# A PSUM pool for the scores, and the q and k projections in the common ring: an attention kernel on one core

## The chip, the core and the metric

The kernel runs on one core of one Trainium2 chip. The metric is the device time of one execution in microseconds (us). Times come from several executions of the compiled program; the profile comes from one further execution, taken by the hardware profiler. The engines are called PE (matmul), PEld (PE's weight loads), DVE, ACT, POOL and SP (which issues DMAs).

## What is computed

For x of 8 batches x 512 tokens x 128 channels in f32, the output is x plus two functions of xn, the layer norm of x:

```
x + rel_attention(xn) + local_transformer(xn)

rel_attention: 16 heads of 8 dims, causal, with a table of relative
               positions for keys and one for values
local_transformer, 6 times:
    y = shift_tokens(x)                 # half of the channels one token back
    q, k, v = split(y @ Wqkv)           # 16 heads of 64 dims
    q, k = l2norm(q) * qs, l2norm(k) * ks, then rotary with scales
    sim = 8 * q k^T in windows of 32: each looks at itself and the one before
    x = x + softmax(sim) v @ Wo
    z = layernorm(shift_tokens(x)) @ W1 ; a, gate = split(z)      # 341 wide each
    x = x + (a * gelu(gate)) @ W2
```

## The kernel before, in words

`rel_attention` does the first part, up to about 560 us of the span. Everything after it, and a beginning that runs beside the end of it, is `steps_of_layers`: 6 layers x 8 batches x 4 tiles of 128 tokens, one tile after another. The state `xt` stays in SBUF, transposed (channels on the partitions). A **batch** here is four tiles and one feed-forward.

A tile passes through these steps. The letters are those of the written order further down.

- `p0` to `p3`, `project` (from L739): half of q, of q, of k, of k. Three matmuls into one bank, `qk_ps` (L637 to L639: the operands are split in a high and a low part, and `product` adds three of the four products). DVE reads the bank twice (`q` L762, `rot` L763), ACT once (`sq`, L764). After the second half, POOL adds `q` and `rot` (L767) and sums of squares are made: for q by POOL L769 and DVE L770, for k by DVE L772, both into `ss`.
- `r`, `normalise` (L777): DVE makes the reciprocal root of `ss` (L782, then L70 to L81; an intermediate, `root_ps`, lies in PSUM too), and POOL multiplies q and k by it (L786).
- `q0 q1 k0 k1`, `turn` (L800): four transposes on PE into one bank, `qkT_ps` (L805), and a copy by ACT into `qT` or `kT` (L808).
- `s0 s1`, `scores` (L810): a matmul that writes the mask into one bank, `sc_ps` (L824), and 32 pairs of small matmuls on top (L836). DVE takes the maximum (L844) and ACT eight exponentials out of the bank, each with its sum (L857). After `s1` DVE inverts the sums (L873), POOL multiplies (L874) and DVE transposes (`pT`, L876).
- `v0` to `v3`, `values` (L881): `product` with Wv and Wo joined, into `v_ps`; a copy by ACT (L890), and four DMAs from SP (L892) that put it in rows of windows, `vw`.
- `a0 a1`, `attend` (L897): matmuls of `vw` and `pT` into `y_ps` (L910), which is held from `a0` to `a1`; a copy by ACT, `ys` (L921).
- `+`, `add` (L924): a transpose into `yT_ps` (L928), added to `xt` by DVE in two parts (L931).
- `f`, `feed_forward` (from L933), once a batch, in stages: the mean over channels by two matmuls with ones (`mean_ps`, L945 and L946; L945 therefore starts once a batch), DVE L947, the square by ACT L949, `var_ps` L953, the reciprocal root by DVE on 4 columns (L76 to L81, then `rstd_hi` L965 and `rstd_lo` L966), `dg` by POOL (L971, twice), `rstd_ps` L978, DVE L986 and L990, ACT L989; then `gate_ps` and `val_ps` (three of each, by `product`), ACT's gelu `h` (L1001), DVE L1011, the split of `h` (ACT L625, POOL L626), `f_ps` by nine matmuls (L1026), and DVE's add to `xt` (L1035, twice). In the last layer `fin_ps` (L1045) follows.

At a layer's end the next layer's weights come by DMA and are split into high and low parts: ACT makes the high parts (L625), DVE most of the low ones (L626, among them `wqk_lo`).

**Orders.** PE's order is written by hand. It is the table ORDERS (L48 to L53), one row for each tile of a batch, run under `tc.manual_schedule`. The first and third rows read

```
"p0 p1 v0 f s0 w2 + p2 f p3 q0 f f q1 s1 w2 k0 v1 w1 a0 r a1 w1 k1 v2 v3"
"p0 p1 s0 w2 v0 v1 f p2 q0 q1 p3 s1 w2 k0 w1 + a0 r a1 w1 k1 v2 v3"
```

In step n of the loop, `p` and `r` belong to tile n + 2, `q` and `k` to tile n + 1, `s` and `v` to tile n, `a` to tile n - 1 and `+` to tile n - 2; `w` loads or splits weights. The orders of DVE, ACT and POOL are not written: the builder's planner chooses them as it builds, from its own model of the timeline, and it also chooses which buffer of a pool a tile takes.

**Banks.** PSUM has eight banks here, and each tile named `..._ps` takes one. `PSB = (2, 6)`. Two banks are the pool `b_qk` (L596), for `qk_ps` alone. Six are the pool `b_x` (L1085), a ring under the one tag `x`, for everything else: `sc_ps`, `qkT_ps`, `v_ps`, `y_ps`, `yT_ps`, the feed-forward's tiles and the roots'. The first instruction that writes a tile waits for the last one that reads the tile which had the bank before (`reuse_waits="tile"`). `rel_attention` has banks of its own while it runs; `b_x` is opened when these are free. Until then `steps_of_layers` has `b_qk` and, through the dictionary `spare`, a pool of `rel_attention` for roots. It projects the first two tiles in that time.

Of the kernel before, what the change touches and what calls it, by code (L numbers as in the profile page):

```python
# [11 lines left out]
F32 = mybir.dt.float32  # L12
# [6 lines left out]
PSUM = bass.MemoryType.PSUM  # L19

P = 128
# [20 lines left out]
H, D = 16, 64  # L42
INNER = H * D
W = 32
# [9 lines left out]
PSB = (2, 6)  # L54
VAR = {'Z': '', 'N': '', 'C': '0', 'D': 1, 'hl': 'P', 'xl': 'P', 'fl': 'P', 'v': 'AAAA', 'q': 'AA', 'k': 'AA', 'pr': 'P', 'R5': 0, 'lo2': 'V'}
NW = P // W
# [526 lines left out]
def local_layers(tc, i, ident, ident_b, xt, out, spare):  # L583


    with ExitStack() as ctx:
        yield from steps_of_layers(ctx, tc, i, ident, ident_b, xt, out, spare)


def steps_of_layers(ctx, tc, i, ident, ident_b, xt, out, spare):  # L590
    nc = tc.nc

    def pool(name, bufs, **kw):
        return ctx.enter_context(tc.tile_pool(name=name, bufs=bufs, reuse_waits="tile", **kw))

    ps_qk = pool("b_qk", PSB[0], space=PSUM, side="right")  # L596
    wp = pool("b_w", 2, side="right")
    w1p = pool("b_w1", 1, side="right")
    w3p = pool("b_w3", 3, side="right")
# [4 lines left out]
    def eng(c):  # L604
        return nc.gpsimd if c == "P" else nc.vector
# [4 lines left out]
    def in_turn(step):  # L610


        ins = step.ins
        if "any" in last:
            tc.add_manual_dep(
                ins,
                last["any"].name,
                mybir.DependencyInfo(mybir.DependencyClass.NoSync, mybir.DependencyReason.DATA),
                reason="one table at a time",
            )  # L620
        last["any"] = ins
# [11 lines left out]
    def product(ps, lhs, rhs):  # L633


        (ah, al), (bh, bl) = lhs, rhs
        nc.tensor.matmul(ps, lhsT=ah, rhs=bh, start=True, stop=False)  # L637
        nc.tensor.matmul(ps, lhsT=ah, rhs=bl, start=False, stop=False)  # L638
        nc.tensor.matmul(ps, lhsT=al, rhs=bh, start=False, stop=True)  # L639
# [96 lines left out]
    def halves(xs, t):  # L736
        return [x[:, t * P : (t + 1) * P] for x in xs]

    def project(n, c):  # L739

        part, a = divmod(c, 2)
        l, b, t = tiles[n]
        if c == 0:
            ready[n] = {"ss": pq.tile([P, 2, H], F32, name="ss")}
        if a == 0:
            ready[n][part] = [
                pq.tile([P, H, 2, D // 2], F32, name="q", bufs=4),
                pq.tile([P, H, 2, D // 2], F32, name="rot", bufs=3),
                pq.tile([P, 2, H, D // 2], F32, name="sq"),
            ]  # L750
        q, v, sq = ready[n][part]
        xs, w, ss = streams[l, b], projections[l, part], ready[n]["ss"]
        cos, sin = (
            tables[l, t][:, 2 * part + m, :].rearrange("p (a d) -> p a d", a=2) for m in range(2)
        )

        def wide(x):
            return x.unsqueeze(1).to_broadcast([P, H, D // 2])

        ps = ps_qk.tile([P, H, D // 2], F32, name="qk_ps")  # L760
        product(ps.rearrange("p h d -> p (h d)"), halves(xs, t), w[a])
        nc.vector.tensor_mul(q[:, :, a], ps, wide(cos[:, a, :]))  # L762
        nc.vector.tensor_mul(v[:, :, 1 - a], ps, wide(sin[:, 1 - a, :]))  # L763
        nc.scalar.activation(sq[:, a], ps, AF.Square)  # L764
        if a == 0:
            return
        nc.gpsimd.tensor_add(q, q, v)  # L767
        if str(part) in VAR["C"]:
            nc.gpsimd.tensor_add(sq[:, 0], sq[:, 0], sq[:, 1])  # L769
            nc.vector.tensor_reduce(ss[:, part, :], sq[:, 0], AX.X, ALU.add)  # L770
        else:
            nc.vector.tensor_reduce(  # L772
                ss[:, part, :], sq.rearrange("p a h d -> p h a d"), AX.XY, ALU.add
            )
        ready[n][part] = q.rearrange("p h a d -> p h (a d)")
# [34 lines left out]
    def scores(n, p):  # L810


        t = tiles[n][2]
        if p == 0:
            probs[n] = {
                "pr": p2.tile([P, 2, 2, NW, 2 * W], F32, name="pr"),
                "mx": p2.tile([P, 2, 2, NW], F32, name="mx"),
                "sm": p2.tile([P, 2 * 2 * NW], F32, name="sm"),
            }
        pr, mx, sm = (probs[n][k] for k in ("pr", "mx", "sm"))  # L820
        qT, kT = turned[n]["q"], turned[n]["k"]
        mask = masks[:, 0 if t == 0 else 1].rearrange("p w k -> p (w k)")
        ps = ps_x.tile([P, 2, NW, 2 * W], F32, name="sc_ps", tag="x")
        nc.tensor.matmul(  # L824
            ps.rearrange("p g w k -> p g (w k)"),
            lhsT=ident_b,
            rhs=mask.unsqueeze(1).to_broadcast([P, 2, NW * 2 * W]),
            start=True,
            stop=False,
            skip_group_check=True,  # L830
        )
        r = slice(D * p, D * p + D)
        for g in range(2):
            for w in range(NW):
                for j in range(4):
                    nc.tensor.matmul(  # L836
                        ps[32 * j : 32 * j + 32, g, w, :],
                        lhsT=qT[r, 4 * g + j, W * w : W * w + W],
                        rhs=kT[r, 4 * g + j, W * w : W * w + 2 * W],
                        start=False,  # L840
                        stop=(g, w) == (1, NW - 1),
                        skip_group_check=True,
                    )
        nc.vector.tensor_reduce(mx[:, p], ps, AX.X, ALU.max, negate=True)  # L844
        if str(p) in VAR["Z"]:
            nc.vector.tensor_add(
                pr[:, p], ps, mx[:, p].unsqueeze(3).to_broadcast([P, 2, NW, 2 * W])
            )
            in_turn(nc.scalar.activation(pr[:, p], pr[:, p], AF.Exp))
        for g in range(2):  # L850
            for w in range(NW):
                if str(p) in VAR["Z"]:
                    continue
                m = (2 * p + g) * NW + w
                kw = {} if str(p) in VAR["N"] else dict(accum_out=sm[:, m : m + 1])
                in_turn(
                    nc.scalar.activation(  # L857
                        pr[:, p, g, w, :],
                        ps[:, g, w, :],
                        AF.Exp,  # L860
                        bias=mx[:, p, g, w : w + 1],
                        **kw,
                    ),
                )
        if str(p) in VAR["Z"] + VAR["N"]:
            nc.vector.tensor_reduce(
                sm[:, 8 * p : 8 * p + 8], pr[:, p].rearrange("p g w k -> p (g w) k"), AX.X, ALU.add
            )
        if p == 0:
            return  # L870
        del turned[n]
        flat = pr.rearrange("p a g w k -> p (a g w) k")
        nc.vector.reciprocal(sm, sm)  # L873
        eng(VAR["pr"]).tensor_mul(flat, flat, sm.unsqueeze(2).to_broadcast([P, 16, 2 * W]))  # L874
        pT = p2.tile([P, 2, 2, NW, 2, W], F32, name="pT")
        nc.vector.transpose(  # L876
            pT.rearrange("p a g w b q -> p (a g w b q)"), pr.rearrange("p a g w k -> p (a g w k)")
        )
        probs[n] = pT
# [193 lines left out]
    for n in range(2):  # L1073
        for c in range(4):
            project(n, c)
            if c == 3:
                normalise(n)
            yield
# [3 lines left out]
    p2 = pool("b_p2", 2)  # L1082
    p3 = pool("b_p3", 3)
    vp = pool("b_vw", 9)
    ps_x = pool("b_x", PSB[1], space=PSUM)  # L1085
    spare.update(pool=ps_x, tag="x")


    mask_f = p1.tile([P, 2, NW, 2 * W], F32, name="mask_f", tag="fsq")
# [11 lines left out]
    with tc.manual_schedule(engines={nc.tensor.engine}):  # L1101
        for n in range(-1, len(tiles) + 2):
# [10 lines left out]
            for step in ORDERS[n % NT].split():  # L1113
# [8 lines left out]
                elif kind == "r" and more:  # L1122
                    normalise(n + 2)
                elif kind == "q" and have(n + 1):
                    turn_q(n + 1, k)
                elif kind == "k" and have(n + 1):
                    turn_k(n + 1, k)
                elif kind == "s" and have(n):
                    scores(n, k)
                elif kind == "v" and have(n):  # L1130
                    values(n, k)
                elif kind == "a" and have(n - 1):
                    attend(n - 1, k)
                elif kind == "+" and have(n - 2):
                    add(n - 2)
                    l, b, t = tiles[n - 2]
                    if t == NT - 1:
                        if l not in weights:
                            weights[l] = load(l)
                        feeding = feed_forward(l, b, weights[l])  # L1140
                elif kind == "f":
                    next(feeding, None)
                elif kind == "w":

                    if have(n + k) and tiles[n + k][1:] == (0, 0):
                        next(making, None)
# [95 lines left out]
```

## Time and profile before

| | us |
|---|---|
| six runs | 3543.26 to 3552.78 |
| median of them | 3549.32 |
| the profiled execution | 3547.9 |
| its span, from the first to the last instruction | 3546.2 |

All shares are of the span. PE is busy for 94% of it, PEld for 71%, DVE for 86%, ACT for 81% and POOL for 83%; TensorE's granted clock is 0.98 in the mean. In an ordinary stretch of 60 us in the layers (2221 to 2281 us) PE is busy 58.80 us, PEld 45.78, DVE 53.72, ACT 52.37 and POOL 54.89, at a granted clock of 1.00.

Rows of the waits view read "engine, line <- releaser: us in all, times, longest": the engine stood still ahead of that line's instruction, and the releaser's end let it go. Rows of the timeline read "start, length, engine, line, operation, output <- inputs, shapes", with the idle time ahead of it and its releaser in brackets. The chain is followed back from the last instruction, at each step to what released it; its shares say on which engine the time of that one path lies.

### The profile page before, as it was taken

To read this page: it belongs to the slowest core of one execution; us is meant where nothing else is said; L and a number is where in the kernel's file an instruction comes from. 1 tells how busy PE (TensorE), PEld (TensorE's weight loads), DVE (VectorE), ACT (ScalarE), POOL (GpSimd) and SP (SyncE) were. 2 spreads that over 40 slices of the span, in tenths; PEclk is the share of its full clock that TensorE was granted. 3 is DMA by queue.
4 is the path that set the end of the run, shared out by engine and by line. 5 is a ranking of instruction groups with operands and counts; after the bars stand their busy time and mean duration, and the time that the engine had idled before them with its cause. 6 is when DMAs were issued, how large, how long until landed. Compare 5 with 4: busy or idle time off the path is not lost.

```text
span 3546.2 us, 130156 instructions
## 1 busy us (share of the span) xinstructions
PE 3347.9 (94%) x49936; PEld 2527.7 (71%) x49936; DVE 3057.6 (86%) x7108; ACT 2861.7 (81%) x9980; POOL 2954.7 (83%) x2274
## 2 busy tenths in 40 slices
PE   6999988999999999999999999998999999999997
PEld 4666656777677777777777777776777777777775
DVE  8888757889888988989898898988989898888894
ACT  3776657888888888788989779897888888888885
POOL 5666667999888999898999789998889998888884
PEclk9999989999999999999999999999999999999998
DMA  1111122223333323333233332323323233232332
GB/s 42 35 29 41 31 62 73 71 73 74 79 84 72 76 71 76 90 76 73 70 76 75 87 77 71 75 71 85 81 73 75 73 75 87 73 77 74 84 75 58
DMA packets 221056, 249.89 MB, mean 70 GB/s; under 512 B 73238, under 2 KB 115604, under 8 KB 220436
## 3 DMA queue, kind: packets, MB, share of 16 engines
q1 hardware_dynamic: 220148, 241.18, 27.7%
q8 instruction: 396, 6.49, 0.8%
q14 instruction: 224, 1.84, 0.2%
q10 hardware_dynamic: 288, 0.39, 0.0%
HBM read 26.92 MB, written 4.19 MB: 9 GB/s over the span
## 4 chain that ended last, share of the span: by engine, by line
PE 38%; ACT 18%; POOL 12%; DVE 9%; issue 3%; DMA 2%; SPq 1%; ACTq 0%; POOLq 0%; DVEq 0%
ACT pr L857 6%; PE qkT_ps L805 6%; PE sc_ps L836 5%; PE y_ps L910 5%; POOL q L786 4%; PE v_ps L637 3%; PE qk_ps L637 3%; PE v_ps L638 3%; PE v_ps L639 3%; POOL pr L874 2%; PE f_ps L1026 2%; PE qk_ps L639 2%; PE qk_ps L638 2%; ACT sq L764 2%; POOL q L767 2%
## 5 line engine op out<-in xcount | busy, mean ns | idle before, releaser
L767 POOL TENSOR_TENSOR q<-q,rot 128x1024 f32<-128x1024 f32 x384 | 922.5, 2402 | 116.7 <-DVE rot L763 90.3
L857 ACT ACTIVATE pr<-sc_ps,mx 128x64 f32<-128x64 f32 x3072 | 926.9, 352 | 111.5 <-DVE mx L844 106.4
L786 POOL TENSOR_TENSOR q<-q,rn 128x1024 f32<-128x1024 f32 x384 | 723.4, 1905 | 29.0 <-DVE rn L81 29.0
L857 ACT ACTIVATION_READ_ACCUMULATOR pr<-sc_ps,mx 128x1 f32 x3072 | 734.8, 245 | 0.0
L764 ACT ACTIVATE sq<-qk_ps 128x512 f32<-128x512 f32 x768 | 477.8, 631 | 227.8 <-DVE rot L763 208.3
L762 DVE TENSOR_TENSOR q<-qk_ps,wrot 128x512 f32<-128x512 f32 x768 | 523.4, 682 | 41.4 <-PE qk_ps L639 31.2
L763 DVE TENSOR_TENSOR rot<-qk_ps,wrot 128x512 f32<-128x512 f32 x768 | 521.6, 679 | 0.0
L890 ACT COPY v<-v_ps 128x512 f32<-128x512 f32 x768 | 471.6, 664 | 45.0 <-DMA vw<-v 20.2
L874 POOL TENSOR_TENSOR pr<-pr,sm 128x1024 f32<-128x1024 f32 x192 | 365.9, 1906 | 152.9 <-DVE rn L78 87.4
L805 PE MATMUL qkT_ps<-ident,q 128*128 128x128 f32 x3072 | 480.5, 283 | 9.5 <-POOL q L786 6.2
L836 PEld LDWEIGHTS sc_ps<-kT,qT 64*32 64x32 f32 x24576 | 363.7, 108 | 126.5 <-issue 126.1
L805 PEld LDWEIGHTS qkT_ps<-ident,q 128*128 128x128 f32 x3072 | 349.8, 142 | 115.3 <-POOL q L786 25.0
L836 PE MATMUL sc_ps<-kT,qT 64*32 64x64 f32 x24576 | 426.3, 219 | 0.0
L910 PE MATMUL y_ps<-vw,pT 128*32 128x128 f32 x11904 | 381.4, 275 | 3.8 <-DMA vw<-v 3.1
L637 PE MATMUL qk_ps<-wqk_hi,xs_hi 128*128 128x512 f32 x768 | 340.2, 443 | 38.7 <-ACT sq L764 38.1
L910 PEld LDWEIGHTS y_ps<-vw,pT 128*32 128x32 f32 x11904 | 327.4, 110 | 57.7 <-issue 42.0
L637 PE MATMUL v_ps<-wvo_hi,xs_hi 128*128 128x512 f32 x768 | 339.8, 442 | 19.8 <-DVE xt L931 10.2
L639 PE MATMUL qk_ps<-wqk_hi,xs_lo 128*128 128x512 f32 x768 | 310.8, 405 | 0.0
L638 PE MATMUL qk_ps<-wqk_lo,xs_hi 128*128 128x512 f32 x768 | 309.5, 403 | 0.0
L639 PE MATMUL v_ps<-wvo_hi,xs_lo 128*128 128x512 f32 x768 | 304.3, 396 | 0.0
L638 PE MATMUL v_ps<-wvo_lo,xs_hi 128*128 128x512 f32 x768 | 302.6, 394 | 0.0
L844 DVE TENSOR_REDUCE mx<-sc_ps 128x8 f32<-128x512 f32 x384 | 260.3, 678 | 23.6 <-PE sc_ps L836 18.4
(207 smaller groups left out, 7602.1 us busy)
## 6 DMA issues: line engine op xcount, KB each, us to landing
vw<-v SPq DMA_DIRECT2D x3072, 64.0 KB
a_qz<-a_qT SPq DMA_DIRECT2D x128, 64.0 KB
wqk_raw<-in_Wqk SPq DMA_DIRECT2D x24, 256.0 KB
wv_raw<-in_WvT SPq DMA_DIRECT2D x12, 256.0 KB
wo_raw<-in_Wo SPq DMA_DIRECT2D x12, 256.0 KB
wrot<-in_trig SPq DMA_DIRECT2D x24, 128.0 KB
a_x<-in_x SPq DMA_DIRECT2D x8, 256.0 KB
a_res<-in_x SPq DMA_DIRECT2D x8, 256.0 KB
```

Source lines behind the costliest of these rows:

```text
L637: nc.tensor.matmul(ps, lhsT=ah, rhs=bh, start=True, stop=False)
L638: nc.tensor.matmul(ps, lhsT=ah, rhs=bl, start=False, stop=False)
L639: nc.tensor.matmul(ps, lhsT=al, rhs=bh, start=False, stop=True)
L762: nc.vector.tensor_mul(q[:, :, a], ps, wide(cos[:, a, :]))
L763: nc.vector.tensor_mul(v[:, :, 1 - a], ps, wide(sin[:, 1 - a, :]))
L764: nc.scalar.activation(sq[:, a], ps, AF.Square)
L767: nc.gpsimd.tensor_add(q, q, v)
L786: nc.gpsimd.tensor_mul(q, q, r[:, m, :].unsqueeze(2).to_broadcast([P, H, D]))
L805: nc.tensor.transpose(tr[:, m, :], q[:, 2 * hp : 2 * hp + 2, :].rearrange("p h d -> p (h d)"), ident)
L836: nc.tensor.matmul(ps[32 * j : 32 * j + 32, g, w, :], lhsT=qT[r, 4 * g + j, W * w : W * w + W], rhs=kT[r, 4 * g + j, W * w : W * w + 2 * W ...
L857: nc.scalar.activation(pr[:, p, g, w, :], ps[:, g, w, :], AF.Exp, bias=mx[:, p, g, w : w + 1], **kw,),
L910: nc.tensor.matmul(y[W * w : W * w + W, :], lhsT=pT[:, p, g, w, half, :], rhs=v[:, p, g, :], start=(p, g, half) == (0, 0, 0 if keys[w] is ...
```

## The change

The scores get a pool of two banks, `b_sc`, and the projections of q and k take their banks from the ring of six, `b_x`, with all else. For the first two tiles, which are projected before `b_x` exists, the old pool of two is opened as before and closed again ahead of the new pools. PSB stays (2, 6). No instruction is added or taken out, and PE's written order stays.

```diff
@@ -593,7 +593,11 @@
-    ps_qk = pool("b_qk", PSB[0], space=PSUM, side="right")
+
+    first = ExitStack()
+    spare["qk"] = first.enter_context(
+        tc.tile_pool(name="b_qk", bufs=2, reuse_waits="tile", space=PSUM, side="right")
+    )
     wp = pool("b_w", 2, side="right")
...
@@ -757,7 +761,7 @@
-        ps = ps_qk.tile([P, H, D // 2], F32, name="qk_ps")
+        ps = spare["qk"].tile([P, H, D // 2], F32, name="qk_ps", tag=spare.get("tag", "qk"))
         product(ps.rearrange("p h d -> p (h d)"), halves(xs, t), w[a])
...
@@ -820,7 +824,7 @@
-        ps = ps_x.tile([P, 2, NW, 2 * W], F32, name="sc_ps", tag="x")
+        ps = ps_sc.tile([P, 2, NW, 2 * W], F32, name="sc_ps")
...
@@ -1082,8 +1086,10 @@
     vp = pool("b_vw", 9)
+    first.close()
+    ps_sc = pool("b_sc", PSB[0], space=PSUM)
     ps_x = pool("b_x", PSB[1], space=PSUM)
-    spare.update(pool=ps_x, tag="x")
+    spare.update(pool=ps_x, qk=ps_x, tag="x")
```

Lines of the changed kernel stand 4 further down from L600 on, and 6 further down from L1090 on.

## The prediction

> **What bounds the kernel now.** I read the page first, then the waits, then one ordinary batch and one layer boundary in the timeline. The page's first and fourth parts:
>
> ```profile
> PE 3347.9 (94%) x49936; PEld 2527.7 (71%) x49936; DVE 3057.6 (86%) x7108; ACT 2861.7 (81%) x9980; POOL 2954.7 (83%) x2274
> ...
> PE 38%; ACT 18%; POOL 12%; DVE 9%; issue 3%; DMA 2%; SPq 1%; ACTq 0%; POOLq 0%; DVEq 0%
> ```
>
> No engine is the bound alone. PE is the busiest, yet the chain that ended last lies on it for 38% only: work is handed round four engines. What the change can act on is the time in which PE has its operands and waits for a bank. The waits view (us in all, times, longest):
>
> ```profile
> PE qk_ps L637 <- ACT sq L764: 38.1, 25, 3.6
> PE mean_ps L945 <- ACT pr L857: 34.3, 20, 3.8
> PE sc_ps L824 <- ACT pr L857: 20.5, 47, 1.7
> PE v_ps L637 <- DVE xt L931: 10.2, 30, 0.5
> ```
>
> In each row a tile's first matmul waits for the last reader of the tile that had its bank: `qk_ps` for the square of the `qk_ps` two before, `mean_ps` and `sc_ps` for the exponentials that read an old `sc_ps`, `v_ps` for the residual add that read `yT_ps`. Together 103.1 us, 2.9% of the span: the most that banks can be worth.
>
> The first part, up to about 560 us, has none of it. Then come 48 batches (6 layers x 8). The starts of L945, once a batch, give the periods: 59.4 to 60.2 us in 30 ordinary batches; 69.4, 64.1 and 66.4 us in the three batches round each of the 5 layer boundaries; 62.25 us in the last layer. In the ordinary batch from 2221 to 2281 us the windows give PE 58.80 us busy of 60, DVE 53.72, ACT 52.37, POOL 54.89. PE idles 1.2 us there, all of it bank waits.
>
> That does not make PE the bound, because the period closes on itself without PE. The timeline (start, length, instruction, idle before and what ended it):
>
> ```profile
> 2214.42 1.25 DVE L876 STREAM_TRANSPOSE pT<-pr 128x1024 f32<-128x1024 f32 x1 [0.78 <-POOL pr L874]
> ...
> 2234.36 1.22 DVE L772 TENSOR_REDUCE ss<-sq 128x16 f32<-128x1024 f32 x1 [0.46 <-ACT sq L764]
> ...
> 2236.84 1.04 POOL L971 TENSOR_TENSOR dg<-ident,rstd_hi 128x512 fp32r<-128x512 f32 x1 [1.88 <-DVE rstd_hi L965]
> ...
> 2248.56 0.69 DVE L770 TENSOR_REDUCE ss<-sq 128x16 f32<-128x512 f32 x1 [0.58 <-POOL sq L769]
> ...
> 2251.98 1.91 POOL L874 TENSOR_TENSOR pr<-pr,sm 128x1024 f32<-128x1024 f32 x1 [1.11 <-DVE rn L78]
> ```
>
> DVE's transpose waited for POOL's product; DVE then runs on to `q` and `rot`, for which ACT's square waits (1.41 us at 2218.42); ACT runs on to the sum that DVE waits for at 2234.36; DVE's `rstd_hi` releases POOL at 2236.84; POOL's `sq` releases DVE at 2248.56, whose `rn` chain releases POOL at 2251.98; POOL then runs without a gap to the next transpose's input, at about 2274.35, one period after the first row. Every step is an engine at work or a wait on another of these three. PE's bank waits stand beside this ring, not in it.
>
> At the boundaries DVE is late, from splitting the next layer's weights (`wqk_lo` L626 4.13 us at 2450.15, others behind it); PE's long waits follow from that:
>
> ```profile
> 2458.43 0.79 PE L637 MATMUL qk_ps<-wqk_hi,xs_hi 128*128 128x512 f32 x1 [3.56 <-ACT sq L764]
> ...
> 2471.45 0.50 PE L945 MATMUL mean_ps<-fx_hi,ones 128*128 128x512 f32 x1 [3.65 <-ACT pr L857]
> ...
> 2583.46 0.38 PE L824 MATMUL sc_ps<-masks,ident_b 128*128 128x512 bf16 x1 [1.71 <-ACT pr L857]
> ...
> 2602.12 0.79 PE L945 MATMUL mean_ps<-fx_hi,ones 128*128 128x512 f32 x1 [3.29 <-ACT pr L857]
> ```
>
> **The change part by part.** No instruction is added or removed, so no engine's sum moves. PE's and SP's orders are the same, instruction by instruction, before and after; so no DMA is moved past another. What moves is the owner of each bank, and what the builder's planner makes of it on the three engines without a written order: on DVE 953 of 7110 instructions by at most 10 places, on ACT 160 of 6912 and on POOL 26 of 2279, these two at layer boundaries and the start.
>
> *Waits removed.* I laid the new succession of banks over the times of before: for each tile, the end of the last read of the bank's previous tile against the start of its own first write. `sc_ps` then has at least 6.8 us to spare, where now 46 of 369 tiles have none; `mean_ps` at least 2.4 us in ordinary batches; `v_ps`'s wait on the residual add goes too. That is about 0.3 (sc) + 0.38 (mean) + 0.44 (v) = 1.1 us of PE's time in an ordinary batch. What is late next: for the scores it is the data, since the copy of `kT` that the second half of L836 reads ends at about 2269.40, which leaves 0.24 us of the 0.30; for the rest it is the ring above. By the ring none of the 1.1 us reaches the period.
>
> *Waits added.* The same table shows where a tile's new predecessor is read too late: in all 26 us over the span (transposes behind a square 31 x 0.28 = 8.8; `y_ps` behind a transpose's copy 4.2; `qk_ps` behind `y_ps`, which is held through both halves of the attention, 3.8; others 2.4, 2.3, 2.3 and below). In an ordinary batch it is `qkT_ps` 38.7 us after the mean, by 0.27 us, in some batches also `y_ps` or `yT_ps`, by 0.4. Behind the waiting transpose on PE stand the rest of that order up to the next mean; who waits for these are the copy of `qT` on ACT and the scores. As PE runs 0.4 to 0.8 us ahead by then from the waits removed, I cost this at nothing; without that cover it is up to 26 us in all.
>
> *Orders.* In an ordinary batch the moved DVE instructions are the 4-wide ones behind the feed-forward's standard deviation: of `ss` L772, L80, two L931, L782, L81, L70, `rstd_hi` L965, the new order has L81 ahead of the L931s and L965 ahead of L70. By the rows' lengths `rstd_hi` ends at 2236.40 instead of 2236.59, and POOL waits for it (1.88 us, on the ring): 0.19 us. The `rn` chain starts later by about as much, which has POOL's `dg` between. Bounds: 0 and 0.25 us. I take 0.19 x 30 = **5.7 us**.
>
> *Boundaries.* Here PE has to wait for DVE's work anyway, and only pieces come through: 0.45 us where `qk_ps` can start once the old `y_ps` is copied (2471.56 instead of 2472.04), 0.36 us where the scores at 2583.46 are let go by the copy of `kT` instead of by exponentials (2584.05 limits it), 0.5 to 0.9 us where `mean_ps` is out of the way before 2602.12: 1.5 us. Below it is nothing (DVE sets all); above, the four waits shown are 12.2 us and 38% of that, PE's share in the chain, is 4.6 us. Times 5: 0 to 23, I take 1.5 x 5 = **7.5 us**, since DVE's row is the nearest.
>
> A row beside it: in the windows 2461 to 2481 and 2581 to 2601 us the granted clock is 0.90 and 0.91 and PE issues 242 and 237 matmuls, against 395 at clock 1.00 from 2481 to 2501. [...]
>
> *Last layer and start.* In the last layer PE keeps the end from 3337 us on; six batches gain 0.3 to 0.6 us less new waits of up to 0.6 us (`qk_ps` behind `y_ps`), which the table places ahead of idle time: I take 0.4 x 6 = **2.4 us**, bounds 0 and 5. The first two tiles keep their own two banks; the planner's other order there is within 2 us either way, taken as nothing.
>
> The sum is 5.7 + 7.5 + 2.4 = 15.6 us, against the profiled execution's own 3547.9 us (span 3546.2 and 1.7 around it): 3532.3. The median of the six runs is 1.4 us higher, 3549.3, which gives 3533.7. I say 3533. Bounds: 0 to 7.5 + 23 + 5 = 35.5 us.
>
> **The rivals.** *PE sets the period.* For it: 98% busy in the ordinary batch, idle only at bank waits, 38% of the chain. Against it: the ring, and PEld at 71%. [...] If so, an ordinary batch gains 1.1 less 0.27 = 0.8 us: 0.8 x 30 + 23 at the boundaries + 5 = 52 us, 3497 (3487 to 3507).
>
> *Nothing comes through:* the ring holds everywhere, DVE sets the boundaries and the new DVE order only shifts a wait: 3543 to 3553, about 3549.
>
> *Slower.* One mechanism: the projections, which had two banks to themselves, now share with `y_ps` and with transposes, so that a square late on ACT holds up a transpose, whose copy is on the same ACT behind it; ACT is part of the ring. Its price is the 26 us of the table, 3549 + 26 = 3575 at most, and 3557 if a third comes through. It decides where PE's lead at the 38.7-us transpose is under 0.27 us, that is, if the removed waits give PE no lead because the ring takes it back first.
>
> **How the numbers follow.** About 0.2%, 7 us, is what a measurement of this kernel can tell from no change. The forecast case (3512 to 3542) has 0.50, PE's period 0.18, nothing 0.18, slower 0.14. So faster 0.68, same 0.18, slower 0.14. The range leaves out half of PE's case (0.09) and the upper two thirds of slower (0.09): 3497 to 3559. The likeliest case's own is 3512 to 3542.
>
> **What would show it.** `PE sc_ps` and `PE mean_ps` must go from the waits, and `PE v_ps <- DVE xt` with them; `qkT_ps <- ACT sq` should come in at about 0.3 us a batch or less. The starts of L945 should be 59.2 to 60.0 us apart in ordinary batches; under 59 would show PE's case, over 60.3 the slower one. At the boundaries the three periods should sum to about 198 us instead of 199.9. The prediction is wrong if DVE's wait for POOL before the transpose (0.78 us) vanishes while the period shortens: then the ring was not the bound.

## The result, and the profile after

The changed kernel takes 3564.5 us (median of 20 runs, 3556.6 to 3580.4), the kernel before 3549.3 us (44 runs, 3541.6 to 3563.6). The ratio is 1.0047, 95% interval [1.0037, 1.0057]: slower by 15 us, where 16 us less were forecast. The profiled execution of the changed kernel took 3578.8 us (span 3577.0), near the upper end of its runs; so its trace shows the mechanisms, and its sums are larger than those of a usual run.

Here are the engines and the waits of PE after (engine, line waited for, releaser: us in all, times, longest):

```profile
PE 3388.3 (95%) x49936; PEld 2574.3 (72%) x49936; DVE 3088.4 (86%) x7108; ACT 2862.6 (80%) x9980; POOL 2953.4 (83%) x2274
...
PE 49%; DVE 18%; ACT 15%; POOL 10%; issue 4%; DMA 3%; SPq 1%; ACTq 0%; POOLq 0%; DVEq 0%
```

```profile
PE qkT_ps L809 <- POOL q L790: 32.0, 41, 4.0
...
PE yT_ps L932 <- ACT v L894: 15.5, 5, 3.3
PE qk_ps L641 <- ACT ys L925: 15.0, 5, 3.0
...
PE qk_ps L641 <- ACT kT L812: 11.4, 5, 3.1
PE sc_ps L840 <- ACT kT L812: 10.3, 5, 2.1
PE qkT_ps L809 <- ACT sq L768: 7.4, 13, 4.1
```

The waits that the change was to remove are gone: no `mean_ps` or `sc_ps` waits for exponentials, no `v_ps` for the residual add, and `qk_ps` has one wait of 2.7 us for the square. What comes in their place is of two kinds. Waits with "5 times" are those of the layer boundaries. The largest row is not one of banks at all: the transposes wait for their data, POOL's product q (and the row of `sc_ps` L840 waits for data too, the copy of `kT`).

And one engine sum grew that could not: DVE has the same 7108 instructions and is busy 30.8 us longer. That is the thread. Three groups of DVE whose mean changed (line, engine, operation, output <- inputs, count, busy us in all, mean ns), before and then after:

```profile
L990 DVE SCALAR_TENSOR_TENSOR fx_lo<-fx,wg,fx_hi 128x512 fp32r<-128x512 f32 x48 | 49.1, 1023 | 2.3 <-ACT fx_hi L989 2.3
L965 DVE CAST rstd_hi<-rstd 128x4 fp32r<-128x4 f32 x48 | 16.4, 342 | 0.1
L966 DVE TENSOR_TENSOR rstd_lo<-rstd,rstd_hi 128x4 fp32r<-128x4 f32 x48 | 7.7, 161 | 0.1
```

```profile
L994 DVE SCALAR_TENSOR_TENSOR fx_lo<-fx,wg,fx_hi 128x512 fp32r<-128x512 f32 x48 | 61.7, 1286 | 2.4 <-ACT fx_hi L993 2.4
L970 DVE TENSOR_TENSOR rstd_lo<-rstd,rstd_hi 128x4 fp32r<-128x4 f32 x48 | 50.4, 1049 | 0.1
L969 DVE CAST rstd_hi<-rstd 128x4 fp32r<-128x4 f32 x48 | 8.1, 168 | 1.3
```

A subtraction of 4 columns takes 1.05 us instead of 0.16. The timeline of an ordinary batch shows with what that goes. DVE before, and POOL beside it:

```profile
2236.59 0.17 DVE L965 CAST rstd_hi<-rstd 128x4 fp32r<-128x4 f32 x1
2236.69 0.20 DVE L71 TENSOR_TENSOR root_ps<-root_ps,rn 128x32 f32<-128x32 f32 x1
2236.80 0.16 DVE L966 TENSOR_TENSOR rstd_lo<-rstd,rstd_hi 128x4 fp32r<-128x4 f32 x1
...
2236.84 1.04 POOL L971 TENSOR_TENSOR dg<-ident,rstd_hi 128x512 fp32r<-128x512 f32 x1 [1.88 <-DVE rstd_hi L965]
```

and after:

```profile
2252.13 0.17 DVE L969 CAST rstd_hi<-rstd 128x4 fp32r<-128x4 f32 x1
2252.34 0.19 DVE L70 TENSOR_SCALAR rn<-root_ps 128x32 int32<-128x32 int32 x1
2252.44 1.00 DVE L970 TENSOR_TENSOR rstd_lo<-rstd,rstd_hi 128x4 fp32r<-128x4 f32 x1
2253.37 0.18 DVE L71 TENSOR_TENSOR root_ps<-root_ps,rn 128x32 f32<-128x32 f32 x1
...
2252.38 1.04 POOL L975 TENSOR_TENSOR dg<-ident,rstd_hi 128x512 fp32r<-128x512 f32 x1 [1.23 <-DVE rstd_hi L969]
```

`rstd_hi` releases POOL. Before, `rstd_lo` starts 0.04 us ahead of POOL's product and is done in 0.16 us. After, it starts 0.06 us behind it and ends when POOL's product ends. Call this a collision. `fx_lo` collides in both kernels: in 46 of 48 batches it starts while POOL is at an instruction; before, it is mostly POOL's `q` (36 times), after mostly its `sq` (41), and it takes 1.29 us in the mean instead of 1.02.

How this reaches the period: some 15 us after `rstd_lo` DVE makes the reciprocal root `rn` (L78) that a later product `pr` of POOL needs. Before, DVE has slack on that way, 0.58 us ahead of L770, where it waits for POOL's `sq`. After, the delay eats it, DVE works without a gap from one to the other, and POOL waits for `rn` 1.69 us instead of the 1.11 us shown at 2251.98 above:

```profile
2268.21 1.91 POOL L878 TENSOR_TENSOR pr<-pr,sm 128x1024 f32<-128x1024 f32 x1 [1.69 <-DVE rn L78]
```

This wait is 1.10 to 1.12 us in each of the 20 ordinary periods before and 1.67 to 1.69 in each of them after. So a reordering of a few short instructions, a by-product of the change that the planner made, turned a race that was won by 40 ns into one that is lost by 60 ns, once a batch.

Where the time went, by the starts of the mean's first matmul (one a batch), in us; the last column is the first experiment's, told below:

| stretch | before | after | after without the collision |
|---|---|---|---|
| up to the first batch's mean | 604.9 | 605.4 | 601.7 |
| the next period | 63.3 | 59.7 | 58.4 |
| 20 ordinary periods (4 in each of 5 layers) | 1192.2 | 1198.8 | 1185.3 |
| 20 periods at the 5 layer boundaries | 1305.2 | 1331.8 | 1313.5 |
| 6 periods from the last layer on | 350.4 | 351.1 | 345.2 |

### The profile page after: what moved, and what is told of

Read it like the earlier page. It is cut to its first block, busy times and chain, and to the rows that moved or that the text cites. A ratio compares the mean times of both kernels' runs of the same rounds, so it can differ in the third digit from the quotient of the medians.

```text
span 3577.0 us, 130361 instructions
## 1 busy us (share of the span) xinstructions
PE 3388.3 (95%) x49936; PEld 2574.3 (72%) x49936; DVE 3088.4 (86%) x7108; ACT 2862.6 (80%) x9980; POOL 2953.4 (83%) x2274
## 4 chain that ended last, share of the span: by engine, by line
PE 49%; DVE 18%; ACT 15%; POOL 10%; issue 4%; DMA 3%; SPq 1%; ACTq 0%; POOLq 0%; DVEq 0%
ACT pr L861 6%; PE qkT_ps L809 6%; PE y_ps L914 5%; PE sc_ps L840 5%; POOL q L790 4%; PE qk_ps L641 3%; PE v_ps L641 3%; POOL q L771 3%; PE v_ps L642 2%; PE v_ps L643 2%; PE qk_ps L643 2%; PE qk_ps L642 2%; PE f_ps L1030 2%; PE a_o_ps L467 2%; PE a_sc_ps L366 2%
## 5 line engine op out<-in xcount | busy, mean ns | idle before, releaser
L771 POOL TENSOR_TENSOR q<-q,rot 128x1024 f32<-128x1024 f32 x384 | 936.6, 2439 | 126.5 <-DVE rot L767 74.9
L840 PEld LDWEIGHTS sc_ps<-kT,qT 64*32 64x32 f32 x24576 | 370.7, 109 | 120.8 <-issue 98.8
L840 PE MATMUL sc_ps<-kT,qT 64*32 64x64 f32 x24576 | 441.2, 221 | 14.7 <-ACT kT L812 10.3
L914 PE MATMUL y_ps<-vw,pT 128*32 128x128 f32 x11904 | 402.6, 277 | 11.2 <-DMA vw<-v 3.4
L914 PEld LDWEIGHTS y_ps<-vw,pT 128*32 128x32 f32 x11904 | 345.8, 111 | 72.1 <-issue 39.5
L641 PE MATMUL v_ps<-wvo_hi,xs_hi 128*128 128x512 f32 x768 | 345.2, 449 | 0.0
```

Of the source, the lines that this page charges most:

```text
L840: nc.tensor.matmul(ps[32 * j : 32 * j + 32, g, w, :], lhsT=qT[r, 4 * g + j, W * w : W * w + W], rhs=kT[r, 4 * g + j, W * w : W * w + 2 * W ...
L914: nc.tensor.matmul(y[W * w : W * w + W, :], lhsT=pT[:, p, g, w, half, :], rhs=v[:, p, g, :], start=(p, g, half) == (0, 0, 0 if keys[w] is ...
```

## The experiments

Theory A: the collision of DVE's `rstd_lo` with POOL's product, by the new order, is the loss; the new banks by themselves are no loss. Theory B: the banks' new waits are the loss. Each run's ratio is to the kernel before on the same chip.

**1 and 2. Take the collision away, and leave everything else.** The last step of the feed-forward's reciprocal root writes to PSUM, into a place of `root_ps` that is free by then. `rstd_hi` and `rstd_lo` read it there, so `rstd_lo` has one input from SBUF instead of two. The order of every engine is the changed kernel's, instruction by instruction.

```diff
-    v.scalar_tensor_tensor(y, t, 1.5 * (3 / 8), y, ALU.add, ALU.mult)
+    v.scalar_tensor_tensor(y if last is None else last, t, 1.5 * (3 / 8), y, ALU.add, ALU.mult)
...
-        rsqrt(nc, rstd, ve, vt, p1.tile([P, NT], F32, name="rstd_s"))
+        rsqrt(nc, rstd, ve, vt, p1.tile([P, NT], F32, name="rstd_s"), last=ve)
...
-        nc.vector.tensor_copy(parts[0], rstd)
-        nc.vector.tensor_sub(parts[1], rstd, parts[0].bitcast(F32))
+        nc.vector.tensor_copy(parts[0], ve)
+        nc.vector.tensor_sub(parts[1], ve, parts[0].bitcast(F32))
```

Run 1, on the changed kernel:

> The changed kernel with one operand moved: the last step of the reciprocal root of the feed-forward writes its 4 columns to PSUM (the place of root_ps that is free by then) instead of SBUF, and rstd_hi and rstd_lo read it there. Instructions, orders and banks stay those of the changed kernel. Theory A, a collision of DVE with POOL: in the changed kernel rstd_lo is issued just after POOL has begun its product dg from rstd_hi, and as both of its inputs lie in SBUF it waits for that product (1.00 us instead of 0.16 in the trace). With one input in PSUM it should take 0.16 to 0.25 us again, ordinary batches should fall from 59.93 to 59.3 us, and the kernel from 3564 to 3538 to 3552. Theory B, the banks: the new waits of PE make the kernel slower. Then nothing changes: 3559 to 3569 us.

Measured: 3536.8 us, ratio 0.9972 [0.9962, 0.9983]. That is 28 us under the changed kernel (27 by the ratios) and 11 us under the kernel before, and 1 us past the lower end of theory A's range. The wait of POOL's `pr` for `rn` is 1.11 us again. `rstd_lo`:

```profile
L970 DVE TENSOR_TENSOR rstd_lo<-root_ps,rstd_hi 128x4 fp32r<-128x4 f32 x48 | 7.7, 160 | 0.1
```

The collision went in two ways. In the ordinary batches L70 now starts 0.08 us after `rstd_hi` instead of 0.21, and `rstd_lo` is ahead of POOL's product again (2231.99 against 2232.03 in one of them). In five batches of the last layer it starts 0.11 us into POOL's `pr`, as in the changed kernel, and takes 0.15 us there instead of 1.81. That pair shows what the place of the operand does; the changed kernel, and then run 1:

```profile
3333.80 1.81 DVE L970 TENSOR_TENSOR rstd_lo<-rstd,rstd_hi 128x4 fp32r<-128x4 f32 x1
...
3333.69 1.90 POOL L878 TENSOR_TENSOR pr<-pr,sm 128x1024 f32<-128x1024 f32 x1 [1.77 <-DVE rn_s L76]
```

```profile
3295.04 0.15 DVE L970 TENSOR_TENSOR rstd_lo<-root_ps,rstd_hi 128x4 fp32r<-128x4 f32 x1
...
3294.93 1.91 POOL L878 TENSOR_TENSOR pr<-pr,sm 128x1024 f32<-128x1024 f32 x1 [1.77 <-DVE rn_s L76]
```

Run 2, the same on the kernel before:

> The same move of one operand in the kernel before, where rstd_lo comes 0.04 us ahead of POOL's product and takes 0.16 us. Theory A: nothing to gain, 3545 to 3553 us (same as 3549). Theory B says the same here; if the kernel gets faster by over 7 us the move itself is worth something apart from the collision, and the first run must be read against that.

Measured: 3543.1 us, ratio 0.9987 [0.9975, 0.9999]. It is some 5 us less, 2 us past the lower end of what was expected, and of the periods only those of the last layer are shorter by as much (311.3 to 306.7 us for five). There the kernel before had a collision that I had overlooked: `rstd_hi`, a cast from SBUF to SBUF, started 0.11 us into POOL's product `pr` and waited for it. The timeline of the kernel before:

```profile
3304.18 1.82 DVE L965 CAST rstd_hi<-rstd 128x4 fp32r<-128x4 f32 x1
...
3304.07 1.91 POOL L874 TENSOR_TENSOR pr<-pr,sm 128x1024 f32<-128x1024 f32 x1 [1.91 <-DVE rn_s L76]
```

In run 2 it starts 0.11 us into the same product, and reads PSUM:

```profile
3300.76 0.15 DVE L965 CAST rstd_hi<-root_ps 128x4 fp32r<-128x4 f32 x1
...
3300.65 1.90 POOL L874 TENSOR_TENSOR pr<-pr,sm 128x1024 f32<-128x1024 f32 x1 [1.91 <-DVE rn_s L76]
```

Runs 1 and 2, on one chip, compare the two layouts of banks with neither of these two collisions (`fx_lo` still meets POOL in both): the new one is faster by 6.3 us (3543.1 less 3536.8).

**5 and 6. Put the collision into the kernel before.** Run 2 gets one more 4-wide copy to SBUF between `rstd_hi` and `rstd_lo`. In run 5 nothing reads it; in run 6 `rstd_lo` does. Orders are the same in both.

```diff
         nc.vector.tensor_copy(parts[0], ve)
+        again = p1.tile([P, NT], F32, name="rstd_c")
+        nc.vector.tensor_copy(again, ve)
-        nc.vector.tensor_sub(parts[1], ve, parts[0].bitcast(F32))
+        nc.vector.tensor_sub(parts[1], again, parts[0].bitcast(F32))    # run 6
```

> Control for the next run. The kernel before with the reciprocal root's last step in PSUM, and one more copy of its 4 columns to SBUF between rstd_hi and rstd_lo, which nothing reads; rstd_lo reads PSUM and rstd_hi, so one input from SBUF. All theories: rstd_lo 0.16 to 0.2 us; one instruction of 0.17 us a batch more than in the second run, 48 x 0.17 = 8 us at most: 3540 to 3553 us.

> The same instructions in the same order on every engine with the old banks, but rstd_lo reads the copy, so both of its inputs lie in SBUF, and the copy puts it behind the start of POOL's product. Theory A (the collision alone makes the slowdown, whatever the banks): rstd_lo about 1.0 us in every batch, and 10 to 30 us more than the control (the changed kernel lost 28 against its version without the collision). Theory B (the collision costs only with the new banks, since it delays a square that the ring now waits for): within 7 us of the control.

Measured: run 5 3541.2 us, ratio 0.9985 [0.9971, 1.0000]; run 6 3565.6 us, ratio 1.0053 [1.0036, 1.0071], 24 us more. `rstd_lo` in run 5 and in run 6:

```profile
2235.10 0.15 DVE L968 TENSOR_TENSOR rstd_lo<-root_ps,rstd_hi 128x4 fp32r<-128x4 f32 x1
...
2235.10 1.04 POOL L973 TENSOR_TENSOR dg<-ident,rstd_hi 128x512 fp32r<-128x512 f32 x1 [1.40 <-DVE rstd_c L967]
```

```profile
2247.57 1.04 DVE L968 TENSOR_TENSOR rstd_lo<-rstd_c,rstd_hi 128x4 fp32r<-128x4 f32 x1
...
2247.55 1.04 POOL L973 TENSOR_TENSOR dg<-ident,rstd_hi 128x512 fp32r<-128x512 f32 x1 [1.95 <-DVE rstd_c L967]
```

Same place, same 4 columns; where one input lies differs, and with it the start by 0.02 us. Over each whole trace, `rstd_lo` starts inside an instruction of POOL in 46 of 48 batches of run 5 and never takes over 0.16 us; in run 6 it is 47 of 48, and it takes 1.0 us or more. In 41 of the 46 the start is within 0.01 us of POOL's, too near to say who came first; in the other five, of the last layer, it is 0.34 us into POOL's instruction (0.15 us long) in run 5 and 0.36 us in run 6 (1.56 us long). POOL's wait for `rn` in the ordinary batch is 1.11 us in run 5 and 1.68 in run 6, as before and after. TensorE's granted clock is 0.98 in the median of both runs, so it has no part in the 24 us; the medians of the changed kernel and run 1 agree too, 0.973 and 0.9725. The old banks with the collision are as slow as the changed kernel. Theory B falls.

**12. Take it away in another manner.** POOL makes the product of `rstd_lo` first, so it cannot begin before `rstd_lo` has ended. PE's order stays; the planner also moves some instructions of DVE, ACT and POOL near the boundaries.

```diff
-        for n in range(2):
+        for n in (1, 0):
             nc.gpsimd.tensor_mul(
                 dg[n],
```

> The changed kernel with the collision taken away in another manner: POOL makes the product of rstd_lo first, so its work cannot begin before rstd_lo has ended; nothing moves to PSUM. Theory A: rstd_lo 0.16 to 0.2 us, 3535 to 3553 us (the last layer's rstd_hi may collide as it does before). If the first run's gain came from PSUM operands and not from the collision, 3558 to 3570.

Measured: 3553.2 us, ratio 1.0012 [0.9995, 1.0029]: 11 us of the loss gone, 0.2 us above theory A's range and 5 us below the other's. `rstd_lo` is 0.15 us in the ordinary batches, 1.81 in five of the last layer (it meets POOL's `pr` there, as `rstd_hi` did before). `fx_lo` takes 1.13 us in an ordinary batch, 1.42 in the changed kernel and 0.96 in run 1. The new order has a price of its own: in an ordinary batch POOL's first product starts 0.54 us after `rstd_hi`, where it is 0.24 in run 1. Against run 1 the 20 ordinary periods of the profiles are 4.6 us longer, five of the last layer 4.5 (as between run 2 and the kernel before), and the boundaries 7.3. That the first is POOL's later start was not tried alone.

**8. All eight banks in one ring**, on run 1's kernel. PE's order is run 1's; DVE's differs in 30 places, ACT's in 7.

```diff
-        ps = ps_sc.tile([P, 2, NW, 2 * W], F32, name="sc_ps")
+        ps = ps_x.tile([P, 2, NW, 2 * W], F32, name="sc_ps", tag="x")
...
-    ps_sc = pool("b_sc", PSB[0], space=PSUM)
-    ps_x = pool("b_x", PSB[1], space=PSUM)
+    ps_x = pool("b_x", 8, space=PSUM)
```

> The first run's kernel (changed banks, no collision of rstd_lo) with all eight banks in one ring: scores and projections both in it, no pool apart. If the 1.2 us of bank waits in an ordinary batch were worth anything, a ring that lets every tile take any bank should be at least as good as 2 + 6: 3528 to 3537 us. If the ring without PE sets the ordinary batch, no change there (59.2 to 59.3 us) and only the boundaries differ: 3530 to 3545 us. The planner may reorder DVE again, which the trace must show first.

Measured: 3520.5 us, ratio 0.9922 [0.9904, 0.9940], better than either branch said. In its profile the 20 ordinary periods are 1183.3 us, 0.1 us a batch under run 1; the boundaries are 12 us shorter (1301.6). More freedom of banks gives an ordinary batch nothing further. DVE's waits for POOL ahead of the transposes, whose end was to be the sign against the ring, are 0.7 us a batch before and 0.8 in runs 1 and 8. The ring without PE holds there.

**3, 4, 7, 10 and 11. The boundaries.** DVE makes `wqk_lo` there from two inputs in SBUF (0.7 us in the first layer, 4.1 and 2.5 at a boundary before, mostly 4.3 and 2.5 after). The trace of the kernel before shows what looks like the same collision: 67 of the 72 `wqk_lo` and `fx_lo` start inside an instruction of POOL, and these 67 end 0.5 to 0.6 us after the end of one. Runs 3 and 4 give it to POOL; 7 and 10 also have four buffers for raw weights instead of two; 11 has the buffers alone. Runs 3, 7 and 11 build on run 1's kernel. Run 4 is the kernel before with this edit alone; run 10 is run 2's kernel with both.

```diff
-            split(hi, lo, raw)
+            split(hi, lo, raw, nc.gpsimd)      # wqk: runs 3, 4, 7, 10
...
-            raw = wp.tile([P, 512], F32, name="wqk_raw", tag="raw", bufs=2)
+            raw = wp.tile([P, 512], F32, name="wqk_raw", tag="raw", bufs=4)   # and 5 more: 7, 10, 11
```

> The first run's kernel, and the low parts of the next layer's wqk made by POOL instead of DVE. In both traces these take 0.7 us in the first layer on DVE but 4.3, 2.5, 2.5 and 1.0 at the layer boundaries. Theory A: it is the same collision, DVE waits there for POOL's instructions; on POOL they cost about 1.3 us each (as the rows of the low part of h do), DVE is no longer late, PE's long waits at the boundaries shrink and the clock stays at 1.00: 5 to 10 us less at each boundary, 25 to 45 us less than the first run. Theory C, POOL is part of the ring that sets the period: 4 x 1.3 us more on POOL at each boundary take back what DVE gives; 0 to 15 us slower than the first run.

> The kernel before with the low parts of wqk made by POOL. Theory A: 5 to 10 us less at each of five boundaries, 3500 to 3525 us. Theory C: 3549 to 3564 us. Beside the third run it shows whether the two layouts of the banks differ at the boundaries once DVE is not late there: the same gain in both if not.

> The third run's kernel (no collision of rstd_lo, low parts of wqk on POOL) with four buffers instead of two for raw weights. In the third run's trace PE waited 41.6 us in 6 times for the DMA of wo_raw ahead of wvo_ps. If the raw buffers, which come free later because POOL is later, took the gain at the boundaries, the boundary's second batch falls from 76 us to 63 to 68 and the kernel from 3546 to 3500 to 3520. If POOL itself is the limit there, it stays at 3535 to 3550.

> The seventh run's edits on the banks of before. It compares the two layouts once neither collision is there. The layouts differed by 6.3 us in runs 1 and 2, in which the new banks gained in ordinary batches (-7) and the first (-4) and lost at the boundaries (+7). If the loss at the boundaries comes from PE's clock after waits that DVE's lateness makes, it goes with these, and this kernel is 10 to 20 us slower than the seventh run: 3502 to 3512. If not, 3492 to 3501.

> The first run's kernel with four raw buffers and the low parts of wqk still on DVE. It divides run 7's gain of some 45 us over run 1. If DVE's collisions at the boundary are the cause and the buffers only let them go, buffers alone give under 10 us: 3527 to 3540. If the weights' DMA was late all along, 3490 to 3520.

| run | banks | us | ratio | boundaries, 20 periods in the profile |
|---|---|---|---|---|
| 1 | new | 3536.8 | 0.9972 | 1313.5 |
| 3: wqk_lo on POOL | new | 3545.7 | 0.9998 [0.9986, 1.0009] | 1327.5 |
| 4: wqk_lo on POOL | old | 3563.0 | 1.0051 [1.0036, 1.0066] | 1324.5 |
| 11: four buffers | new | 3505.2 | 0.9894 [0.9858, 0.9930] | 1293.5 |
| 7: both | new | 3492.1 | 0.9841 [0.9818, 0.9863] | 1282.7 |
| 10: both | old | 3511.5 | 0.9899 [0.9870, 0.9928] | 1282.7 |

Runs 3 and 4 missed what theory A said of the boundaries, which are longer than in run 1 and in the kernel before. Their times, 8.9 us over run 1 and 3563.0 us, lie in theory C's ranges. But run 3's trace names a wait that theory C does not have:

```profile
PE wvo_ps L724 <- DMA wo_raw<-in_Wo: 41.6, 6, 8.4
```

With POOL later, the raw buffers come free later, and the next weights' DMA with them. Run 7 gives them room: that wait is 0.5 us in its trace, and the run is 45 us under run 1, 8 us below the range expected. So theory C's numbers were hit, in part at least, for another reason. Run 11 missed what I held likelier, that the buffers alone are worth under 10 us: they give 30, which the other branch had named; in its profile 20 are at the boundaries and 13 before the first batch. Run 7 is 13 us under run 11, but with four runs of each their intervals just overlap: that the late loads counted is shown, that DVE's waiting at the boundaries did is likely.

Runs 7 and 10 set the layouts side by side once more: the boundaries are equal, where the new banks lost 7.5 us in runs 1 and 2 (1313.5 against 1306.0), and the new layout is 0.58 points of ratio, some 20 us, ahead. In the profiles it gains 11.7 us in the ordinary periods and 8.6 before the first batch; why more than in runs 1 and 2 was not tried. Run 10's time lies in the branch that put the loss at the boundaries down to PE's clock, which fits that cause but does not show it.

**9. Everything together**: run 7 with run 8's single ring.

> All that helped together: one ring of eight banks, the reciprocal root's last step in PSUM, low parts of wqk on POOL, four raw buffers. If the gains are independent (run 8 is 0.5 points of ratio under run 1, run 7 1.3 points), the ratio is about 0.979 and the time 3470 to 3482 us. If ring and POOL's part act on the same waits at the boundaries (run 7 and run 8 both shorten these), 3482 to 3495.

Measured: 3495.0 us, ratio 0.9852 [0.9820, 0.9884]. No better than run 7 (0.9841), which fits the second branch: the ring's gain and run 7's lay at the same boundaries. Its six runs spread from 3482 to 3517 us, so the two can't be told apart. Run 7 has the lowest time found, 1.6% under the kernel before.

## Why the prediction was wrong

**What bounds the kernel: right, as far as it was tried.** The ring of DVE, ACT and POOL sets the ordinary batch. The bank waits of about 1.1 us a batch went. Without the collision the 20 ordinary periods fell from 1192.2 to 1185.3 us, 0.35 us each; a ring of eight banks added 0.1. PE got no lead from it: its gaps of over 0.05 us are 0.7 us in an ordinary batch before and 0.9 in run 1, where it waits for POOL's q instead.

**Waits removed and added: right in kind; the whole was too large, the new waits too small.** Like for like (runs 1 and 2) the change is worth 6.3 us, where the sum said 15.6 (runs 7 and 10: some 20). The new waits for banks were to be 26 us in all; four rows of run 1 alone are 57 (`yT_ps` behind `v` 16.5, `qk_ps` behind `ys` 16.0 and behind `kT` 11.4, `qkT_ps` behind the square 13.3), most of it at the boundaries. The rival "slower" had a price of up to 26 us that nearly hits the measured loss, for another reason: its mechanism, the ring's new waits, is not what cost the time.

**Orders: the step that failed.** It is "No instruction is added or removed, so no engine's sum moves", and with it the term for the new order, 5.7 us of gain with "Bounds: 0 and 0.25 us" a batch. The prediction had the new place of `rstd_hi` before it and priced it by lengths from the rows of before. The gain itself came: `rstd_hi` starts 2.03 us after the start of L772's sum instead of 2.23. But it took the length of `rstd_lo` as given and did not ask what POOL would be doing when it starts; the term could not be negative. Measured: DVE's sum 30.8 us more, `rstd_lo` 0.84 us longer in an ordinary batch, `fx_lo` 0.26 us longer in the mean, `rn` 0.8 us later where "about as much" as 0.19 was said, and 0.67 us more for an ordinary period (1198.8 against 1185.3 over 20). In the medians the collision costs 28 us with the new banks and 24 with the old. Two slips besides: 2236.59 is the start of `rstd_hi` in its row, not its end, and 24 periods lie between 59.2 and 60.5 us, not 30, so the term should have been 4.6 us. The profile of before showed the sign to look for: `fx_lo` 0.74 to 1.5 us and `wqk_lo` 0.7 to 4.1 us for the same shape; the five that start beside no instruction of POOL take 0.68 to 0.75 us, the other 67 up to 4.1.

What in the hardware makes DVE wait beside POOL was not shown. What was: with one input in PSUM `rstd_lo` never takes over 0.16 us in run 5, where it starts inside an instruction of POOL in 46 batches; with both in SBUF it takes 1.0 us or more in 47 batches of run 6.

**Boundaries: wrong in sign for the layout itself.** Forecast 7.5 us of gain. The 20 periods rose by 8.3 us without the collision (1305.2 to 1313.5) and by 26.6 with it. The prediction priced three periods at a boundary, 199.9 to about 198 us, and run 1 has 198.2 in the mean; that was luck in part, since the second of them is 5.6 us longer and the first and third 2.5 and 4.6 shorter. The fourth, which the sum left out, rose by 3.2 us. PE's waits there changed place, not size: run 1's four at a boundary are 3.3, 3.3, 2.6 and 2.1 us, 11.3 in all, against 12.2. What grew is the time at half clock after them: over the 20 boundary periods the clock records give 79 us before and in run 2, 130 in run 1 and 150 in the changed kernel. The window view of the changed kernel (window, length, then busy us and count for PE, PEld, DVE, ACT, POOL, then the granted clock):

```profile
1966.00:1970.00 4.00, 1.29 (x6) 0.72 (x4) 4.00 (x6) 2.44 (x17) 1.51 (x2) 1.00 0.44 111
1970.00:1978.00 8.00, 7.26 (x103) 5.41 (x106) 7.91 (x10) 5.42 (x12) 4.51 (x3) 0.57 0.23 70
1978.00:1982.00 4.00, 4.00 (x52) 3.35 (x46) 3.97 (x5) 1.06 (x5) 3.39 (x3) 1.00 0.39 114
1982.00:1986.00 4.00, 1.81 (x6) 0.78 (x4) 3.45 (x14) 3.76 (x18) 1.61 (x1) 0.85 0.50 147
1986.00:1998.00 12.00, 12.00 (x100) 10.24 (x99) 7.06 (x16) 6.15 (x24) 7.58 (x5) 0.50 0.33 81
```

and of the kernel before at the same boundary:

```profile
1955.00:1959.00 4.00, 0.69 (x4) 0.22 (x2) 4.00 (x6) 3.21 (x18) 1.91 (x1) 1.00 0.37 111
1959.00:1964.00 5.00, 4.71 (x78) 3.75 (x78) 4.95 (x7) 2.92 (x6) 2.13 (x2) 0.66 0.33 105
...
1968.00:1972.00 4.00, 0.78 (x4) 0.30 (x2) 3.80 (x9) 2.21 (x15) 1.61 (x2) 1.00 0.53 148
1972.00:1978.00 6.00, 5.68 (x80) 4.30 (x81) 5.62 (x14) 3.11 (x8) 5.37 (x3) 0.72 0.44 120
```

Two idle stretches in each; before, half clock lasts 3.41 us each time (from 1960.00 and from 1973.65), after, the second time, it stays at 0.50 for all of the 12 us from 1986 on, in which PE is never idle. Over 21 runs of the changed kernel the time goes with the mean granted clock (0.967 to 0.977; correlation -0.88, about 24 us for 0.01). That these waits bring on the longer stretch, and that it makes the boundaries longer, is argued from the traces, not shown: no run held the waits and changed the clock. Runs 7 and 10 speak against a simple count: 85 and 58 us at half clock, and equal boundaries.

**Last layer: right.** Forecast 2.4 us; run 1 against run 2, 1.4 us over five periods (306.7 to 305.4) and 2.2 from there to the end. **First batch:** taken as nothing; the first full period is 4.4 us shorter (62.7 in run 2 to 58.4 in run 1).

## What to carry to other kernels

A change that adds no instruction can still lengthen them, here DVE's by 30.8 us in all. Where a planner reorders, look at each moved DVE instruction of the kinds that collided here, a subtraction with both inputs in SBUF (`rstd_lo`, 0.16 us before and 1.05 in the mean after) or a cast from SBUF to SBUF (`rstd_hi`, in the kernel before 0.17 us in an ordinary batch and 1.82 beside `pr`), and at what POOL runs beside its new place; lengths from the old trace were no guide to it. If an engine's sum of busy time grows with the same instructions, compare the means group by group before reading any wait. And where a short instruction wins or loses such a race by some tens of ns, try an operand in PSUM: here that added no instruction, `rstd_lo` took 0.15 us instead of 1.81 beside the same `pr`, and it was worth 28 us where 46 of 48 batches collided, 5 us where only the last layer did.

## What the runs showed of the hardware that was not expected

PE at work without a gap stayed at half clock for 12 us (1986 to 1998 us after), where the stretch just before ended after 6.8. In the traces of the kernels before and after the clock records hold full and half clock alone, and each stretch at half clock that ends within the span (30 before, 33 after) is a whole multiple of 3.41 us long; this one is 13.65 us, four of them. A 4-wide subtraction with both inputs in SBUF took 1.04 us and ended 0.02 us after POOL's instruction, although it started only 0.02 us behind it (run 6); with one input in PSUM it took 0.15 us, started 0.34 us behind one (run 5). One DVE instruction was passed by POOL's next: `wqk_lo` at 2450.15 in the kernel before starts 0.18 us into a `q` of POOL and ends, after 4.13 us, 0.55 us behind the end of the `pr` that follows that `q`.
